# Cross-attention, 32 batches on one core: the first batch's split of queries and keys made by VectorE instead of accumulating transfers, and the set-up's order rewritten

## The chip, the core and the metric

The kernel runs on one core of a Trainium2 chip. The core has five engines with a queue of instructions each: PE (TensorE, matrix products into PSUM), DVE (VectorE), ACT (ScalarE), POOL (GpSimd) and SP (SyncE, which here only issues transfers). Each engine works through its queue in order and waits on semaphores for the others and for transfers. The metric is the device time of one execution in microseconds. All times below are in microseconds unless ns is written; those inside a profile count from the start of its span.

## The reference

`x` and `y` (called `ctx_2048`) are 32 x 256 x 1024 in float32, the weights 256 x 256. For each batch:

```python
x_q = einsum('oc,bcn->bno', w_qk, y)
x_k = einsum('oc,bcn->bon', w_qk, x)
x_v = einsum('oc,bcn->bon', w_v, x) + b_v
energy = einsum('bnc,bcm->bnm', x_q, x_k)            # 1024 x 1024
attention = softmax(energy, axis=-1)
attention = attention / (1e-07 + attention.sum(axis=1, keepdims=True))
x_r = einsum('bcn,bnm->bcm', x_v, attention)
x_r = relu(einsum('oc,bcn->bon', w_t, x - x_r) + b_t)
return x + x_r
```

Softmax runs over rows of the energy, the second normalisation over its columns.

## The kernel before

**Folded weights.** The energy is `y^T (w_qk^T w_qk) x`, so the kernel forms `G = w_qk^T w_qk` once (tile `g`) and per batch only `G x`, the *keys* (name `g` in tiles, class `Keys`). In the same way `w_t w_v` is folded into one matrix (tile `wvtT`, made by `value_weights`) for the *values* `u` (class `Values`), and `w_t` is turned by `turned_weights` (tile `wtT`). `value_bias` makes the bias `bu` of the values: DVE spreads `b_v` into `bvs` (inside `scratch`), PE multiplies (`pb`), ACT copies, and also negates `b_t` to `nbt`.

**Seven products.** Each product of 2 x 2 blocks is done with seven block products and not eight (class `Seven`). Block sums of the weights are made by DVE in `lefts` (tiles `gs`, `wtTs`, `wvtTs`, four scalar_tensor_tensor each, after ACT's copies of the PSUM banks), block sums of `x` in `summed` (tile `xs`: GpSimd's tensor_tensor for batch 0; for later batches two loads by SP and three accumulating transfers by GpSimd, `xsteps`). Three PSUM banks `one`, `two`, `three` collect the products: `p1`, `p5`, `p2` begin them; `p6`, `p7`, `p4` go on in `one`, `p3` in `two`. Between them ACT keeps copies (`p1s`, `p5s`, `w`). `c11`, `c12`, `c22` (DVE, one tensor_tensor of 128x512 each) and `c21` (an ACT copy) put the four blocks of the result together. For keys the result is `gfr`, two tiles of 128x1024 (block rows 0 and 1); for values it is `ut`. As all products but three go on in a bank that is read meanwhile, the order is tied: `p6` waits for the copy `p1s`, `p7` for the copy `w`, `p4` for `c22`'s reading, `c21` for `p4`.

**The split.** The energy needs more than one pass of the fast matrix form. Class `Split` keeps each of `y` (tile `yf`, from rows `yfr`) and the keys (tile `gf`, from `gfr`) in three forms of 128 x 2 x 1024 in fp32r: `high` (the value, scaled), `low` (what `high` lacks) and a third, `both`, that mixes the two. With `i` the block row, 0 or 1, `parts(i)` has ACT write `high`, and scaled copies of it to the places of `low` and `both`; `lower(i)` is a transfer of GpSimd's queue that adds the rows to `low`; `mixed(i)` is another that adds `low` to `both`, after the first has landed. So a batch has twelve ACT passes of 128x1024 and eight accumulating transfers of 512 KB.

**Energies.** Class `Energy` works on one of eight row tiles `n`. `products(h)` issues six matmuls `pe` of 128x512 for each half `h`: `high` by `high` and `low` by `low` into one bank, `both` by `both` into another, for `i` of 0 and 1. `gather(h)`: ACT scales the first bank into `es`, DVE's custom instruction adds the second bank, writes `e` and the running minimum `nm`. `exp` (ACT) follows one row later, `share` (DVE: a reciprocal and the addition into `acc`, the column sums) two rows later. After the last row, `columns` and `inverse` (DVE) make the column factors `rc`. Then class `Attention` scales `e` (DVE) and multiplies (PE, `po`). Before the attention of batch b the keys and values of batch b+1 are made, and their split.

**Order.** The class `InOrder` (lines 62 to 78) wraps PE, DVE, ACT and POOL so that each keeps the order in which the program is written; only waits move an instruction. SP's transfers go in the order written too. PSUM is one pool of eight banks, and buffers of `rowp` (four: the two `yfr` and two `gfr` of a batch) are reused when their last reader is done. So the order of the set-up, lines 631 to 673, is the order of every queue before the loop. At row 0 of batch 0 (lines 690 to 703) the values' `p4` and `c21` follow, then `xsteps[1]` and `[2]`, then `factors` on GpSimd: two additions of `bu` to `ut` and four block sums `us`.

In the trace all operations that go through `InOrder` carry one line (L73), so they are told apart by tiles.

Of the kernel before, what the change touches and what calls it, by code (L numbers as in the profile page):

```python
# [12 lines left out]
ALU = mybir.AluOpType  # L13
# [4 lines left out]
def kernel(  # L18
# [25 lines left out]
    KC = C // P  # L44
# [9 lines left out]
    UP = 4096.0  # L54
    UNDER = 1.0 - 2.0**-13
# [22 lines left out]
    pe, dve, act, pool = (InOrder(g) for g in (nc.tensor, nc.vector, nc.scalar, nc.gpsimd))  # L78

    def bank(name):  # L80
        return ps_m.tile([P, MB], F32, tag="m", name=name)
# [61 lines left out]
    def lefts(name, ps, sign=1.0):  # L143


        w = const.tile([P, KC, C], F32, name=name)
        for k in range(KC):
            act.mul(w[:, k, :], ps[k][:, :C], sign)
        sums = const.tile([P, 4, P], F32, name=f"{name}s")
        s1, s2, s3, s4 = (sums[:, j] for j in range(4))  # L150

        def stt(out_, block, factor, other, op):
            dve.scalar_tensor_tensor(out_, block, factor * sign, other, ALU.mult, op)

        p11, p12, p21 = ps[0][:, :P], ps[1][:, :P], ps[0][:, P:C]
        a11, a12, a21, a22 = w[:, 0, :P], w[:, 1, :P], w[:, 0, P:], w[:, 1, P:]
        stt(s1, p21, 1.0, a22, ALU.subtract)
        stt(s3, p11, 1.0, a21, ALU.subtract)
        stt(s2, p11, -1.0, s1, ALU.add)
        stt(s4, p12, 1.0, s2, ALU.add)  # L160
        return w, (a11, a12, s4, a22, s1, s2, s3)
# [10 lines left out]
    def turned_weights():  # L172

        pt = [bank(f"pt_{i}") for i in range(KC)]
        for i in range(KC):
            for k in range(KC):
                pe.transpose(pt[i][:, ts(k, P)], wt[:, k, ts(i, P)], ident)
        return lefts("wtT", pt)

    def value_weights(wtT):  # L180

        pw = [bank(f"pw_{i}") for i in range(KC)]
        for i in range(KC):
            for k in range(KC):
                pe.matmul(
                    pw[i][:, :C], wv[:, k, ts(i, P)], wtT[:, k, :], start=(k == 0), stop=(k == KC - 1)
                )
        return lefts("wvtT", pw, -1.0)[1]

    def value_bias(wtT):  # L190

        pb = bank("pb")
        for k in range(KC):
            dve.tensor_scalar(bvs[:, k], few, bv[:, k], None, ALU.add)
        for k in range(KC):
            pe.matmul(pb[:, :C], bvs[:, k], wtT[:, k, :], start=(k == 0), stop=(k == KC - 1))
        act.mul(bu.rearrange("p k c -> p (k c)"), pb[:, :C], -1.0)
        act.mul(nbt[:, :, 0], bt[:, :, 0], -1.0)
# [13 lines left out]
    def value(v):  # L212

        return v.bitcast(F32)

    def summed(b):

        s = up.tile([P, 4, MB], F32, tag="xs", name=f"xs_{b}")
        t1, t3, t4, t2 = (s[:, j] for j in range(4))
        to = loaded[b]  # L220
        b11, b12 = to[:, 0, ts(0, MB)], to[:, 0, ts(1, MB)]
        b21, b22 = to[:, 1, ts(0, MB)], to[:, 1, ts(1, MB)]
        if b == 0:
            pool.tensor_tensor(t1, b11, b12, ALU.add)
            pool.tensor_tensor(t2, b22, t1, ALU.add)
            pool.tensor_tensor(t3, b12, b22, ALU.add)
            pool.tensor_tensor(t4, b21, t2, ALU.add)
            steps = []
        else:
            q = quarters(x[b])  # L230
            nc.sync.dma_start(s[:, :2], q[:, 0, 1:2, :].to_broadcast([P, 2, MB]))
            nc.sync.dma_start(s[:, 2:], q[:, 1])
            steps = [
                lambda: accumulate(s[:, :2], corners(x[b])),
                lambda: accumulate(s[:, 2:], s[:, 0:1].to_broadcast([P, 2, MB])),
                lambda: accumulate(t4, q[:, 1, 1]),
            ]
        return (b11, b21, b22, t4, t1, t2, t3), steps

    class Split:  # L240
# [12 lines left out]
        def parts(self, i):  # L253

            high, low, both = (self.to[:, j, i] for j in range(3))
            act.mul(high, self.rows[i], UNDER * self.by)
            act.mul(low, value(high), -1.0 / self.by)
            act.mul(both, value(high), -1.0 / (UP * self.by))

        def lower(self, i):  # L260
            accumulate(value(self.to[:, 1, i]), self.rows[i])
# [370 lines left out]
    q = Queries(0)  # L632
# [4 lines left out]
    g = Keys(0, xr)  # L637
    g.p1()
    g.p5()
    g.p2()  # L640
    g.p6()
    wtT, t_left = turned_weights()
    g.p3()
    g.p7()
    u_left = value_weights(wtT)
    value_bias(wtT)
    for i in range(KC):
        q.parts(i)
        q.lower(i)
    g.c11()  # L650
    g.c12()
    g.split.parts(0)
    g.split.lower(0)
    g.c22()
    g.p4()
    g.c21()
    g.split.parts(1)
    g.split.lower(1)
    for i in range(KC):
        q.mixed(i)  # L660
        g.split.mixed(i)
    xn, xsteps = summed(1)
    xsteps[0]()
    u = Values(0, xr)
    u.p1()
    u.p5()
    u.p2()
    u.c11()
    u.p6()
    u.p3()  # L670
    u.c12()
    u.p7()
    u.c22()

    before = None
    for b in range(B):
# [34 lines left out]
        if more:  # L711
            q = Queries(b + 1)
            for i in range(KC):
                q.load(i, nc.sync.dma_start)
            g = Keys(b + 1, xn)
# [33 lines left out]
        if more:  # L749
# [33 lines left out]
            xr, u = xn, un  # L783
# [34 lines left out]
```

## Time and profile before

| what | value |
|---|---|
| time, median of 3 runs | 2130.79 (2130.71 to 2130.84) |
| the profiled execution's own time | 2130.66 |
| its span | 2128.9 |
| mean granted clock of PE | 0.994 |
| first pe matmul | 35.39 |
| pe running without a break, from the second row on | 52.44 |
| first matmul of batch 1's keys | 71.80 |
| first matmul of batch 2's keys | 139.51 |
| first matmul of batch 3's keys | 204.91 |

The span runs from the first to the last recorded instruction of the execution. A row such as `L73 PE MATMUL pe<-gf,yf 128*128 128x512 f32 x3072` is a group: engine, operation, the tile written and the tiles read, sizes, and how many. In an answer in order of time the two numbers ahead are start and length; several like instructions may be merged in one row (then `x` tells how many), and brackets at the end tell how long the engine stood still before it and what released it. In a row on waits the numbers are the total, how often, and the longest.

### The profile page before, as it was taken

The page shows a single profiled execution, that of the slowest core. Times are in us where ns is not written, and L with a number is a line of the kernel's source. Part 1 is how long each engine was busy: PE and PEld are TensorE (multiplying, and loading weights), DVE is VectorE, ACT ScalarE, POOL GpSimd, SP SyncE. Part 2 cuts the span into 40 slices and gives each one's busy share as a digit, 9 for nine tenths or more (in the row PEclk, how much of TensorE's full clock was granted, in tenths as well). Part 3 has the DMA queues.
Part 4 walks back from the last instruction along what each step waited for, and adds up shares of the span by engine and source line. Part 5 has one row for each costly group of instructions (what it writes and reads, how often), then busy time and mean ns, then how long its engine had stood idle before and what let it go on. Part 6 is the DMA issues. An engine that isn't in the chain of part 4 may idle for free.

```text
span 2128.9 us, 23494 instructions
## 1 busy us (share of the span) xinstructions
PE 2087.1 (98%) x7586; PEld 1290.6 (61%) x7586; DVE 1812.7 (85%) x3024; ACT 1179.7 (55%) x1802; POOL 681.3 (32%) x582
## 2 busy tenths in 40 slices
PE   5999999999999999999999999999999999999998
PEld 4666556665556665566655566655666555666564
DVE  1988889888899888898888998888888889988898
ACT  3664556655556645566555566455665555664562
POOL 2333331333332333323333323333233333233321
PEclk7999999999999999999999999999999999999999
DMA  8456766557766567665577665676655776656740
GB/s 206 88 127 163 177 154 129 139 136 181 168 128 145 129 163 178 155 133 134 136 179 167 128 146 128 163 178 150 135 138 135 177 170 127 148 127 162 178 95 30
DMA packets 108954, 310.34 MB, mean 146 GB/s; under 512 B 10784, under 2 KB 11552, under 8 KB 108832
## 3 DMA queue, kind: packets, MB, share of 16 engines
q0 software_dynamic: 58192, 174.87, 44.9%
q1 hardware_dynamic: 50496, 133.85, 18.5%
q8 instruction: 60, 0.98, 0.2%
q14 instruction: 62, 0.51, 0.1%
q10 hardware_dynamic: 144, 0.13, 0.0%
HBM read 124.78 MB, written 33.55 MB: 74 GB/s over the span
## 4 chain that ended last, share of the span: by engine, by line
PE 61%; DVE 29%; issue 4%; ACT 1%; DMA 1%; DVEq 0%; POOL 0%; ACTq 0%; POOLq 0%
PE pe L73 31%; PE po L73 28%; DVE e L73 14%; DVE acc L73 4%; DVE et L73 4%; DVE gfr L73 3%; DVE rc L73 2%; DVE sc L73 1%; PE pu L73 1%; DVE parts L73 1%; ACT es L73 1%; DVE ri L73 0%; DMA gf<-gfr 0%; PE pg L73 0%; DMA gf<-gf 0%
## 5 line engine op out<-in xcount | busy, mean ns | idle before, releaser
L73 PE MATMUL pe<-gf,yf 128*128 128x512 f32 x3072 | 718.7, 394 | 10.9 <-DMA gf<-gf 10.9
L73 PEld LDWEIGHTS pe<-gf,yf 128*128 128x128 f32 x3072 | 578.0, 188 | 145.7 <-issue 27.3
L73 ACT ACTIVATE es<-pe 128x512 f32<-128x512 f32 x512 | 304.2, 595 | 184.7 <-PE pe L73 184.4
L73 PE MATMUL po<-et,us 128*128 128x512 f32 x768 | 353.9, 597 | 11.5 <-DVE et L73 11.5
L73 DVE SCALAR_TENSOR_TENSOR e<-e,ri,rc 128x512 f32<-128x512 f32 x512 | 347.4, 746 | 1.1
L73 DVE SCALAR_TENSOR_TENSOR acc<-e,ri,acc 128x1024 f32<-128x1024 f32 x224 | 289.9, 1294 | 8.0
L73 ACT ACTIVATE e<-e,nm 128x1024 f32<-128x1024 f32 x256 | 292.7, 1143 | 3.4 <-DVE nm L73 3.3
L73 PEld LDWEIGHTS po<-et,us 128*128 128x128 f32 x768 | 142.9, 190 | 207.0 <-issue 158.4
L73 DVE CUSTOM_DVE_ANT_0 e<-pe,es,nm 128x512 f32<-128x512 f32 x256 | 192.2, 751 | 76.5 <-ACT es L73 49.4
L73 PE MATMUL po<-e,ut 128*128 128x512 f32 x512 | 225.0, 592 | 1.0 <-DVE e L73 1.0
L73 POOL DMA_DIRECT2D yf<-yfr x64 | 55.0, 860 | 533.0 <-ACT yf L73 518.6
L73 DVE CUSTOM_DVE_ANT_0 e<-pe,es 128x512 f32<-128x512 f32 x256 | 175.5, 686 | 51.6 <-ACT es L73 39.1
L73 ACT ACTIVATE z<-po,bt 128x512 f32<-128x512 f32 x31 | 21.4, 689 | 337.1 <-DMA out_dram<-z 234.5
L73 PEld LDWEIGHTS po<-e,ut 128*128 128x128 f32 x512 | 97.2, 190 | 123.8 <-issue 107.4
L73 DVE TENSOR_TENSOR et<-e 128x1024 f32<-128x1024 f32 x128 | 153.7, 1221 | 4.4
L73 POOL TENSOR_TENSOR ut<-ut,bu 128x1024 f32<-128x1024 f32 x64 | 153.5, 2473 | 0.0
L73 POOL DMA_DIRECT2D gf<-gf x64 | 54.8, 856 | 306.3 <-DMA gf<-gfr 262.8
L73 DVE SCALAR_TENSOR_TENSOR z<-z,x 128x512 f32<-128x512 f32 x96 | 132.2, 1377 | 3.3
L73 ACT ACTIVATE yf<-yf 128x1024 fp32r<-128x1024 f32 x128 | 128.2, 1049 | 2.0
L73 ACT ACTIVATE gf<-gf 128x1024 fp32r<-128x1024 f32 x128 | 128.2, 1049 | 2.0
L73 PE MATMUL po<-e,us 128*128 128x512 f32 x256 | 125.3, 592 | 0.0
L73 POOL DMA_DIRECT2D xs<-xs x31 | 37.2, 1201 | 248.4 <-DMA xs<-in_x_dram 240.9
(106 smaller groups left out, 2753.7 us busy)
## 6 DMA issues: line engine op xcount, KB each, us to landing
yfr<-in_ctx_dram SPq DMA_DIRECT2D x64, 512.0 KB, 5.8
yf<-yfr POOLq DMA_DIRECT2D x64, 512.0 KB, 5.1
gf<-gfr POOLq DMA_DIRECT2D x64, 512.0 KB, 10.6
yf<-yf POOLq DMA_DIRECT2D x64, 512.0 KB, 8.0
gf<-gf POOLq DMA_DIRECT2D x64, 512.0 KB, 5.2
out_dram<-z SPq DMA_DIRECT2D x128, 256.0 KB, 3.5
x<-in_x_dram SPq DMA_DIRECT2D x31, 1024.0 KB, 7.4
xs<-in_x_dram SPq DMA_DIRECT2D x62, 512.0 KB, 5.1
```

The source lines that it names most:

```text
L73: self.last = getattr(self.engine, name)(*args, **kwargs)
```

## The change

Only code ahead of the loop changes, for batch 0; batches 1 to 31 are issued as before. `Split` gets three new methods. `high(i)` is the ACT pass for `high` as before. `low(i)` is one DVE scalar_tensor_tensor of 128x1024 (`high` times a constant, plus the rows), written straight to the `low` form; `both(i)` is another (`high` times a constant, plus `low`). In the set-up they take the place of `parts`, `lower` and `mixed`: eight ACT passes and eight transfers go, eight DVE instructions come.

The order changes too. The keys' `c11`, `c12`, `c22`, `p4` and `c21` move ahead of `value_weights`, with the passes `high` of `y` among them; `value_weights` stands behind the passes `high` of the keys; the remaining `low` and `both` follow its block sums on DVE; `value_bias` moves behind the values' products `p1` to `p7`; the values' `c11` and `c12` move behind it. `xsteps[0]` on GpSimd's queue is no longer behind eight transfers.

```diff
+        def high(self, i):
+            act.mul(self.to[:, 0, i], self.rows[i], UNDER * self.by)
+
+        def low(self, i):
+            high, low = (self.to[:, j, i] for j in range(2))
+            dve.scalar_tensor_tensor(
+                low, value(high), -1.0 / self.by, self.rows[i], ALU.mult, ALU.add
+            )
+
+        def both(self, i):
+            high, low, both = (self.to[:, j, i] for j in range(3))
+            dve.scalar_tensor_tensor(
+                both, value(high), -1.0 / (UP * self.by), value(low), ALU.mult, ALU.add
+            )
...
     g.p1()
     g.p5()
     g.p2()
+    g.c11()
+    q.high(0)
     g.p6()
+    q.low(0)
     wtT, t_left = turned_weights()
     g.p3()
+    q.high(1)
+    g.c12()
     g.p7()
-    u_left = value_weights(wtT)
-    value_bias(wtT)
-    for i in range(KC):
-        q.parts(i)
-        q.lower(i)
-    g.c11()
-    g.c12()
-    g.split.parts(0)
-    g.split.lower(0)
     g.c22()
+    q.low(1)
     g.p4()
     g.c21()
-    g.split.parts(1)
-    g.split.lower(1)
+    g.split.high(0)
+    g.split.high(1)
+    u_left = value_weights(wtT)
     for i in range(KC):
-        q.mixed(i)
-        g.split.mixed(i)
+        g.split.low(i)
+    for i in range(KC):
+        g.split.both(i)
+    for i in range(KC):
+        q.both(i)
     xn, xsteps = summed(1)
     xsteps[0]()
     u = Values(0, xr)
     u.p1()
     u.p5()
     u.p2()
-    u.c11()
     u.p6()
     u.p3()
+    u.p7()
+    value_bias(wtT)
+    u.c11()
     u.c12()
-    u.p7()
     u.c22()
```

## The prediction

> **What bounds the kernel now.** I read the page first, then the stretches of the set-up, then who waited for whom in it, then the instructions in order of time. The page says that the loop is TensorE's:
>
> ```profile
> PE 2087.1 (98%) x7586; PEld 1290.6 (61%) x7586; DVE 1812.7 (85%) x3024; ACT 1179.7 (55%) x1802; POOL 681.3 (32%) x582
> PEclk7999999999999999999999999999999999999999
> ```
>
> 98% busy, and the granted clock is low only in the first of 40 slices (53 us each): what PE lost lies there, the set-up that the change rewrites. Cut into stretches (span, then busy time and count of PE, PEld, DVE, ACT, POOL, then clock, DMA share, GB/s):
>
> ```profile
> 24.00:35.00 11.00, 4.75 (x22) 4.76 (x23) 1.38 (x2) 7.17 (x10) 4.33 (x5) 0.57 1.03 233
> 35.00:53.00 18.00, 8.02 (x26) 6.06 (x26) 2.15 (x5) 1.37 (x3) 3.29 (x3) 0.60 0.85 157
> 53.00:72.00 19.00, 19.00 (x85) 15.75 (x84) 14.86 (x29) 14.04 (x26) 12.11 (x7) 1.00 0.21 34
> ```
>
> From 24 to 53 us PE is less than half busy at about half clock while the DMA engines are full; from 53 us it never stops. The waits up to 75 us say on what:
>
> ```profile
> PE pe L73 <- DMA gf<-gf: 9.9, 2, 5.4
> PE pu L73 <- ACT up1s L73: 8.8, 1, 8.8
> POOL yf L73 <- ACT yf L73: 11.2, 2, 9.2
> ```
>
> and in order of time (start, length):
>
> ```profile
> 24.12 2.00 ACT L73 ACTIVATE gf<-gf 128x1024 fp32r<-128x1024 f32 x2
> 29.63 0.57 ACT L73 COPY up1s<-pu 128x512 f32<-128x512 f32 x1
> 36.98 0.86 POOL L73 DMA_DIRECT2D gf<-gf  x1 [2.37 <-DMA gf<-gfr]
> 41.55 0.77 PE L73 MATMUL pe<-gf,yf 128*128 128x512 f32 x1 [4.49 <-DMA gf<-gf]
> 47.76 3.32 PE L73 MATMUL pe<-gf,yf 128*128 128x512 f32 x7 [5.44 <-DMA gf<-gf]
> 52.44 19.51 PE L73 MATMUL pe<-gf,yf 128*128 128x512 f32 x84
> 59.50 2.52 DVE L73 TENSOR_SCALAR acc<-e,ri 128x1024 f32<-128x1024 f32 x1
> 81.36 1.25 DVE L73 TRANSPOSE_TENSOR_REDUCE parts<-acc 128x32 f32<-128x1024 f32 x1
> ```
>
> ACT is a chain from 17.09 to 29.7 (twelve passes of 1.05 over yf and gf); GpSimd's transfers wait for its passes (the third wait), and PE's pu waits behind it for one copy, 8.8 us. Then the energies pe wait for the eight accumulating transfers, the last landing just before 47.7. From 52.44 PE runs 84 matmuls (seven rows of twelve, 0.2305 us each) to 71.80, where the next batch's keys begin.
>
> **The change, part by part.**
>
> *Removed:* eight transfers and eight of ACT's passes (8.4 us). With them go PE's 9.9 us of waiting on gf and nearly all of the 8.8 us behind up1s. What is late next is VectorE, which receives eight scalar_tensor_tensor of 128x1024 with two SBUF operands. The nearest row is that of acc<-e,ri,acc: 1.28 us undisturbed, 1.96 and 1.84 at 63.67 and 67.29 beside GpSimd's tensor_tensor. From 12 us to the end of the chain GpSimd only issues transfers, so I take 1.28 for one and 1.20 from start to start (ten of half the size take 6.71, that is 0.67 each for a duration of 0.746).
>
> [...]
>
> *The new chain.* Its first wait is new: ACT's high(0) stands ahead of the copy gw, and yfr_0 lands at 12.3 (issued at 4.14, 8.2 to landing), yfr_1 at 13.5.
> - ACT: high(0) 12.3-13.4, gw to 14.0 (0.59; was over at 10.6), wtT twice to 14.7, high(1) to 15.8.
> - PE: p3 ends at 11.2 as before; p7 goes onto the bank that gw reads, so it moves from 11.1 to 14.05-15.1.
> - DVE: low(0) 13.4-14.7, the four wtTs sums (1.1) to 15.9, c12 and c22 (0.62 apart) to 17.15, low(1) to 18.4. c11 is done by 9.9, in idle time.
> - PE: p4 waits for c22: 17.2. Then pw.
> - ACT: c21 (0.57), the two high passes of gf (2.1), only then the two wvtT copies (0.38 each).
> - DVE: the wvtTs sums (1.1) stand ahead of the six remaining scalar_tensor_tensor, so these wait for wvtT. After them two bvs (0.47); value_bias's matmuls pb need bvs, and every pe is queued behind pb.
>
> *The clock.* Before, a stretch without work at 22.2-25.6 was followed by clock 0.50 from 25.6; a stretch with 1.16 of 3.41 us busy (35.85-39.26) by 0.50; one with 1.83 of 3.37 busy (12.0-15.37) left it at 1.00; a full one (32.4-35.85) brought it back. New gaps: between 11.2 and 17.2 PE does only p7 (1.0 us), and between the end of pu and pb nothing. By these rows both cost half clock afterwards; I take that.
>
> [...]
>
> With half clock: p4 17.2-19.2 and pw (1.89 full, 3.8 half) to 22.7; c21 to 19.8, high of gf to 22.0, wvtT to 22.4 and 23.1; wvtTs to 24.25; six times 1.20 to 31.5; bvs to 32.0. Meanwhile pu, six products 0.9 apart from 22.4, is over by 28, with idle time after it. pb at half clock (1.9) ends at 33.9. Row 0 (twelve pe) then has 1.95 us at half clock, 4.2 matmuls, and 7.8 at 0.231: 37.65. u's p4 (0.9): 38.55. Seven rows, 19.36: **57.9 instead of 71.80, 13.9 us earlier.**
>
> With full clock throughout: pw over at 20.1, wvtT at 21.7, wvtTs 22.8, six to 30.0, bvs 30.5, pb 31.4, row 0 34.2, p4 35.1, rows 54.5: 17.3 earlier. This is the good end. The bad end is VectorE at 1.96 eight times: 5.4 later, 8.5 earlier than now.
>
> *What the rows gain besides.* In the first batch VectorE trailed PE more than later: from the start of the keys (71.80) to the column reduction (81.36) 9.56 us, in the next batch 7.25 (139.51, 146.76). The distance between key starts is 67.71 for the first and 65.40 for the second: the trail cost PE 2.3. Its source is GpSimd, whose six tensor_tensor of u's factors (56.35 to 68.05) stretched acc to 2.52, 1.96 and 1.84 (the means of these forms are 0.81 and 1.29). They start after u's c21. Before, GpSimd was held until 56.35 by the xs accumulations queued behind the eight transfers; now those can go at 18 and are over by about 33, so the factors start at about 39.5, some 3 us earlier against the rows, and cover one share and part of another. Between nothing and 2.3 I take 1.0.
>
> *Costed at nothing:* c11, under the wait for yfr. The next batch's yfr loads, whose slots are freed by low(0) and low(1) instead of the transfers: needed at 83 only, they now start near 18.7 behind xs on SP's queue. nbt and bu move behind pu; bu is due when GpSimd adds it at 39.5 and is over by about 35. If PE ran faster than here, this would be the next wait, off PE's path. u's c11, c12 and c22 (2 us) follow bvs, to 34.2; only u's p4 at 37.65 waits for c22. PSUM: at row 1 a bank may have to wait for u's c21 (0.59), with the first sums' matmuls as cover; 0 to 0.6.
>
> *Sum:* 13.9 + 1.0 = 14.9. The profiled execution took 2130.66 (span 2128.9 and 1.8 around it), against a median of 2130.79, so both are one base: 2130.66 - 14.9 = 2115.8. Say **2116**.
>
> **The rivals.**
> 1. *The clock holds* (other phase, or p7 enough). For: 54% busy kept it. Against: 1.0 in 6 us is far less. 17.3 + 0 to 2.3: 2111 to 2113.
> 2. *VectorE or the queue order costs more*: contention, later yfr, half clock for a stretch more (3.4 us at half, 1.7 lost), no recovered trail. 2118 to 2122.
> 3. *The rows become VectorE's.* A row costs it 0.69 + 0.08 + 0.75 + 0.08 + 0.16 + 1.28 = 3.04 of work against PE's 2.77. Before, it had idle time ahead of row 0; now it comes out of the set-up with u's three sums. If the trail grows by its full 0.27 a row and GpSimd's stretch (2.9) stays whole, 5 of the gain go: 2121. Against: steady batches run so with a trail of 7.
> 4. *Slower.* One mechanism: scalar_tensor_tensor on VectorE stretched 3.2-fold, as z<-z,x at 178.69 shows (2.22 where 0.69 is usual, beside GpSimd). Eight at 4.1 instead of 1.28 add 22.6: 2138. It decides from 3.7 us each (14.9 + 4.3, over eight, on top of 1.28). Against: that row lies beside a tensor_tensor of GpSimd, and the transfers that GpSimd issues from 96.05 to 98.1 leave TENSOR_TENSOR et at 96.29 at 1.23.
> 5. *The transfers were hidden anyway*: no change. PE's 9.9 us wait names them, with 8.8 more behind ACT; little is left for it.
>
> **How the numbers follow.** Forecast (2114 to 2118) 0.55, rival 1 0.15, rival 2 0.16, rival 3 0.07, rival 4 0.04, no change 0.03. A measurement of this kernel tells about 0.2%, 4.3 us. The first four are all faster: 0.93; same 0.03; slower 0.04. The range takes in rival 1 from its full recovery and rivals 2 and 3 to 2121.5, and leaves out the rest: 2111.5 to 2121.5.
>
> **What the profile after would show.** Eight scalar_tensor_tensor of about 1.28 on yf and gf; six of them between 24 and 32; no wait of pe on DMA; ACT idle from 8.9 to 12.3 before yf<-yfr; first pe near 34, continuous to the keys near 58; clock below 1 in the stretches after 15 and after 32; column reduction about 8.5 after the start of the keys, and 65 to 67 from there to the next. The forecast is wrong if the new passes take over 2 us, if pe still stops between rows, or if a gain at 58 is given back by batch 1.

## The result, and the profile after

The changed kernel takes 2112.91 us (median of four executions, 2108.64 to 2113.70) against 2130.75 for the kernel before measured beside it (2130.5 to 2130.84): a ratio of 0.9913, 95% interval 0.9898 to 0.9929. That is 17.8 us less, where 14.9 were forecast. The median lies inside the forecast range of 2111.5 to 2121.5; the execution that was profiled, at 2108.64, lies below it.

From the page of the changed kernel, its engine totals and its clock row:

```profile
PE 2081.3 (99%) x7586; PEld 1286.3 (61%) x7586; DVE 1815.0 (86%) x3032; ACT 1171.9 (56%) x1794; POOL 673.3 (32%) x574
PEclk9999999999999999999999999999999999999999
```

Eight instructions left ACT and eight left GpSimd, eight came to DVE. The clock row alone settles little, since a 9 stands for 0.90 or more; but the mean granted clock of this execution is 1.00, and no part of its first 40 us shows less. The stretches of the set-up, in the columns used before (span; busy time and count of PE, PEld, DVE, ACT, POOL; clock; DMA share; GB/s):

```profile
24.00:35.00 11.00, 8.26 (x49) 7.17 (x49) 7.91 (x14) 3.44 (x7) 5.52 (x4) 1.00 0.44 73
35.00:53.00 18.00, 18.00 (x79) 14.61 (x78) 15.20 (x35) 14.30 (x26) 6.98 (x5) 1.00 0.00 1
53.00:72.00 19.00, 19.00 (x81) 11.36 (x80) 18.33 (x33) 15.29 (x22) 2.58 (x3) 1.00 0.32 55
```

From 35 to 53 us PE was busy for 8.0 us before and is busy for all 18 now, with the DMA engines at rest. Who waited for whom up to 62 us (total, how often, longest):

```profile
DVE wvtTs L73 <- ACT wvtT L73: 3.2, 1, 3.2
PE pb L73 <- DVE scratch L73: 2.7, 1, 2.7
PE pg L73 <- DVE gfr L73: 1.9, 1, 1.9
ACT yf L73 <- DMA yfr<-in_ctx_dram: 1.8, 1, 1.8
PE pg L73 <- ACT gw L73: 1.1, 1, 1.1
PE pu L73 <- ACT wvtT L73: 1.1, 1, 1.1
```

PE's 9.9 us of waiting on transfers of `gf` and its 8.8 us behind `up1s` are gone. What it waits for in their place is small: `p7` for `gw`, `p4` for `c22` (written to `gfr`) and `pb` for VectorE's `bvs` (in `scratch`), all three named in the prediction, and `pu` for `wvtT`. In order of time (start, length):

```profile
11.56 1.06 ACT L73 ACTIVATE yf<-yfr 128x1024 fp32r<-128x1024 f32 x1 [1.84 <-DMA yfr<-in_ctx_dram]
13.23 1.10 PE L73 MATMUL pg<-xs,gs 128*128 128x512 f32 x2 [1.13 <-ACT gw L73]
16.20 1.10 PE L73 MATMUL pg<-xs,g 128*128 128x512 f32 x2 [1.87 <-DVE gfr L73]
21.33 2.35 DVE L73 SCALAR_TENSOR_TENSOR gf<-gf,gfr 128x1024 fp32r<-128x1024 f32 x2
23.59 2.35 DVE L73 SCALAR_TENSOR_TENSOR gf<-gf 128x1024 fp32r<-128x1024 f32 x2
25.87 2.35 DVE L73 SCALAR_TENSOR_TENSOR yf<-yf 128x1024 fp32r<-128x1024 f32 x2
28.56 1.10 PE L73 MATMUL pb<-wtT,scratch 128*128 128x256 f32 x4 [2.74 <-DVE scratch L73]
30.54 2.73 POOL L73 TENSOR_TENSOR ut<-ut,bu 128x1024 f32<-128x1024 f32 x1
33.05 19.30 PE L73 MATMUL pe<-gf,yf 128*128 128x512 f32 x84
39.90 1.09 DVE L73 TENSOR_SCALAR acc<-e,ri 128x1024 f32<-128x1024 f32 x1
52.19 1.02 PE L73 MATMUL pg<-x,g 128*128 128x512 f32 x2
59.10 1.25 DVE L73 TRANSPOSE_TENSOR_REDUCE parts<-acc 128x32 f32<-128x1024 f32 x1
```

The chain is the one in the prediction, link by link: landing of `yfr`, copy `gw`, `p7`, `c22`, `p4`, then VectorE's six forms back to back from 21.33 to 28.14, `pb`, rows. The keys of batch 1 start at 52.19 (before: 71.80), 19.61 earlier. The distance to the next keys (117.25) is 65.06 instead of 67.71, another 2.65. Together 22.26; this execution is 2130.66 - 2108.64 = 22.02 shorter than the profiled one of before. So in this execution the whole gain is made before 117 us; of a lead of 22.4 at the keys near 1030 us, 22.0 is left at the end.

### The profile page after: what moved, and what is told of

Its sections match the earlier page's. It is cut to its first block, busy times and chain, and to the rows that moved or that the text cites. A ratio compares the mean times of both kernels' runs of the same rounds, so it can differ in the third digit from the quotient of the medians.

```text
span 2106.9 us, 23473 instructions
## 1 busy us (share of the span) xinstructions
PE 2081.3 (99%) x7586; PEld 1286.3 (61%) x7586; DVE 1815.0 (86%) x3032; ACT 1171.9 (56%) x1794; POOL 673.3 (32%) x574
## 4 chain that ended last, share of the span: by engine, by line
PE 62%; DVE 29%; issue 4%; ACT 1%; DMA 1%; DVEq 0%; POOL 0%; ACTq 0%; POOLq 0%
PE pe L73 31%; PE po L73 29%; DVE e L73 14%; DVE acc L73 4%; DVE et L73 4%; DVE gfr L73 3%; DVE rc L73 2%; DVE sc L73 1%; PE pu L73 1%; DVE parts L73 1%; ACT es L73 1%; DVE ri L73 0%; DMA gf<-gfr 0%; PE pg L73 0%; DMA gf<-gf 0%
```

## The experiments

All ran against the kernel before on the same chip. The first four share a chip (before: 2130.62), e5 to e8 another (2130.88), e9 a third (2131.35). Unless the text says otherwise, times are medians of four executions. `e1_again` and `e8_again` are the changed kernel itself, so that the others have it on their own chip.

The columns to compare, each from the profiled execution (for "trail": from the keys of batch 1 to the column reduction `parts<-acc`; the last three columns are the first three `share` on `acc`, which take 0.75, 1.28 and 1.28 where GpSimd does not stretch them):

| kernel | time | keys of batch 1 | to the keys of batch 2 | trail | first shares |
|---|---|---|---|---|---|
| before | 2130.75 | 71.80 | 67.71 | 9.56 | 2.52, 1.96, 1.84 |
| changed | 2112.91 | 52.19 | 65.06 | 6.91 | 1.09, 1.29, 1.28 |
| e1_again | 2111.57 | 55.45 | 65.01 | 6.88 | 1.07, 1.28, 1.28 |
| e2_filled | 2109.10 | 51.77 | 65.86 | 7.70 | 1.45, 1.29, 1.28 |
| e3_held_factors | 2114.79 | 56.03 | 67.85 | 9.75 | 2.72, 1.95, 1.84 |
| e4_old_order | 2113.40 | 57.04 | 65.03 | 6.89 | 1.05, 1.28, 1.28 |
| e5_order_transfers | 2128.14 | 69.59 | 68.04 | 9.91 | 2.88, 1.95, 1.84 |
| e6_both_early | 2109.07 | 50.86 | 66.15 | 8.01 | 1.63, 1.84, 1.28 |
| e7_best | 2106.44 | 46.68 | 67.83 | 9.70 | 2.65, 1.96, 1.84 |
| e8_again | 2110.84 | 54.08 | 65.06 | 6.91 | 1.09, 1.28, 1.28 |
| e9_best_factors | 2104.27 | 46.98 | 65.84 | 7.71 | 1.90, 1.28, 1.28 |

### The same kernel again: where is the half clock?

No edit. The first profile had a clock of 1.00 throughout, which the prediction held for the less likely case; its three other executions had a mean granted clock of 0.997.

> The changed kernel as it is, timed more often, because its four runs lie apart (2108.64, 2112.44, 2113.39, 2113.70) where the kernel before lies within 0.4 us. Theory A (the clock): TensorE's clock falls to half in the set-up in some runs and not in others, by where windows of 3.41 us fall against the gaps of the set-up; then times form two groups, about 2108.6 with a mean granted clock of 1.000 and 2112 to 2114 with about 0.997 (0.3% of 2111 us are 6.3 us lost to the clock scale, that is about 12 us at half clock), and a profile with 0.997 shows the half clock between 15 and 40 us. Theory B (the landing of x and yfr): times spread evenly with the landing of yfr_0 and the clock has no part in it; then runs of one clock lie apart by some us as well.

Measured: 2111.57 (2109.94 to 2112.81), ratio 0.9909 [0.9894, 0.9924]; the profiled execution took 2112.81 at a mean clock of 0.998. Its stretches:

```profile
17.00:20.50 3.50, 3.50 (x7) 2.17 (x8) 0.84 (x1) 1.57 (x3) 1.35 (x1) 0.54 0.64 208
27.00:34.00 7.00, 4.25 (x14) 3.33 (x14) 5.01 (x8) 0.80 (x3) 2.66 (x3) 0.76 0.59 95
13.40:17.00 3.60, 1.25 (x3) 0.48 (x4) 3.50 (x8) 1.84 (x4) 0.00 (x0) 0.97 1.03 399
27.00:30.40 3.40, 0.65 (x5) 0.49 (x5) 3.40 (x6) 0.00 (x0) 0.19 (x1) 1.00 0.86 149
```

and PE's instructions there:

```profile
16.85 2.05 PE L73 MATMUL pg<-xs,g 128*128 128x512 f32 x2 [1.88 <-DVE gfr L73]
18.69 2.65 PE L73 MATMUL pw<-wtT,scratch 128*128 128x256 f32 x8
30.17 1.77 PE L73 MATMUL pb<-wtT,scratch 128*128 128x256 f32 x4 [2.75 <-DVE scratch L73]
31.37 4.29 PE L73 MATMUL pe<-gf,yf 128*128 128x512 f32 x12
```

The two half-clock stretches are where the prediction put them: after the gap around `p7` (`p4` takes 2.05 instead of 1.10), and after the gap ahead of `pb` (row 0 takes 4.29 instead of 3.10). But each lasts about 3.4 us, so the first ends near 20.2, inside `pw`: `pw` takes 2.65, not 3.8. The keys start at 55.45, which is 3.26 later than with full clock and 2.45 earlier than the forecast of 57.9.

### The gaps of PE filled

```diff
+    def fill(p, count):
+        for _ in range(count):
+            pe.matmul(p[:, :P], few, few, start=True, stop=True)
...
+    pw = [bank(f"pw_{i}") for i in range(KC)]
+    fill(pw[0], 5)
     g.p7()
+    fill(pw[1], 7)
...
         pb = bank("pb")
+        fill(pb, 11)
```

The extra products multiply a tile of zeros (`few`); what they write is overwritten by `pw` and `pb`.

> As the changed kernel, with small matmuls of zeros (128x128) put into TensorE's three gaps: 5 ahead of the keys' p7, 7 ahead of p4, 11 ahead of pb, into banks that the next product starts anew. Theory A: the clock stays at 1.000 in every run, and all times lie at 2108 to 2110 (up to 1 us more than the best run if the fillers overrun a gap). Theory B: the spread of 5 us stays.

Measured: 2109.10 (2108.88 to 2109.63), ratio 0.9899 [0.9882, 0.9915], with a clock of 1.00 in all four executions. The two stretches that cost e1 its clock:

```profile
13.40:17.00 3.60, 3.33 (x20) 2.42 (x19) 3.23 (x8) 0.86 (x2) 0.43 (x1) 1.00 1.04 404
27.00:30.40 3.40, 3.13 (x18) 2.61 (x17) 3.02 (x6) 0.69 (x3) 0.00 (x0) 1.00 0.90 154
```

PE is now busy for 3.33 of 3.60 and 3.13 of 3.40 (in e1: 1.25 and 0.65), and the clock stays. The spread shrinks from 2.9 us in e1 to 0.75, and the median falls by 2.5. So the gaps cause the half clock, and the half clock most of the spread. Over the twelve executions of the changed kernel (first result, e1, e8) the times go with the mean clock: at 1.0 2108.64, 2109.58 and 2109.94; at 0.998 six between 2110.81 and 2112.81; at 0.997 2112.44, 2113.39 and 2113.70. Three of twelve executions kept the clock without any filling.

### The factors held back

```diff
-                if b == 0:
-                    ur, usteps = u.factors()
-                    for step in usteps:
-                        step()
...
+            if b == 0 and n == 1:
+                pool.tensor_copy(behind, e[:, 1, N - 1 : N])
+                ur, usteps = u.factors()
+                for step in usteps:
+                    step()
```

GpSimd's six tensor_tensor then start only when row 1 of the energies is written, which is the relation to the rows that the kernel before had.

> As the changed kernel, with GpSimd's factors of the first batch held until row 1 of the energies has been gathered, by one copy of a column of e ahead of them. Theory T (the trail): the shares beside GpSimd stretch as in the kernel before (acc 2.52, 1.96, 1.84), the column reduction stands about 9.5 us after the start of the keys and not 6.9, and the time is 2.2 to 2.7 us above the changed kernel in runs of the same clock. Rival: the trail has another cause (VectorE came later to row 0); then nothing changes, within 0.5 us.

Measured: 2114.79 (2111.64 to 2115.16), ratio 0.9921 [0.9907, 0.9936], 3.2 slower than e1 (its one execution at a clock of 1.0 took 2111.64, that of e1 2109.94). In order of time, GpSimd's additions and VectorE's first three shares:

```profile
41.11 4.79 POOL L73 TENSOR_TENSOR ut<-ut,bu 128x1024 f32<-128x1024 f32 x2
43.73 2.72 DVE L73 TENSOR_SCALAR acc<-e,ri 128x1024 f32<-128x1024 f32 x1
47.68 1.29 POOL L73 TENSOR_TENSOR us<-us,ut 128x512 f32<-128x512 f32 x1
48.11 1.95 DVE L73 SCALAR_TENSOR_TENSOR acc<-e,ri,acc 128x1024 f32<-128x1024 f32 x1
48.94 2.27 POOL L73 TENSOR_TENSOR us<-ut 128x512 f32<-128x512 f32 x1
51.17 1.30 POOL L73 TENSOR_TENSOR us<-ut,us 128x512 f32<-128x512 f32 x1
51.71 1.84 DVE L73 SCALAR_TENSOR_TENSOR acc<-e,ri,acc 128x1024 f32<-128x1024 f32 x1
65.78 1.25 DVE L73 TRANSPOSE_TENSOR_REDUCE parts<-acc 128x32 f32<-128x1024 f32 x1
```

The stretched shares of before are back, the second and third almost to the hundredth (2.72, 1.95, 1.84 against 2.52, 1.96, 1.84), with them the trail (9.75) and the distance to the next keys (67.85, 2.84 more than in e1). This is the second part of the gain, made and unmade by the time at which GpSimd's additions run. Another 0.58 stands already ahead of the keys (56.03 against 55.45): the profiled execution of e3 has one 3.4 us stretch of half clock more than that of e1.

### The forms by VectorE in the old order

```diff
-    g.c11()
-    q.high(0)
     g.p6()
-    q.low(0)
     wtT, t_left = turned_weights()
     g.p3()
-    q.high(1)
+    g.p7()
+    u_left = value_weights(wtT)
+    value_bias(wtT)
+    for i in range(KC):
+        q.high(i)
+        q.low(i)
+    g.c11()
     g.c12()
-    g.p7()
+    g.split.high(0)
+    g.split.low(0)
     g.c22()
-    q.low(1)
     g.p4()
     g.c21()
-    g.split.high(0)
     g.split.high(1)
-    u_left = value_weights(wtT)
-    for i in range(KC):
-        g.split.low(i)
-    for i in range(KC):
-        g.split.both(i)
+    g.split.low(1)
     for i in range(KC):
         q.both(i)
+        g.split.both(i)
...
     u.p2()
+    u.c11()
     u.p6()
     u.p3()
+    u.c12()
     u.p7()
-    value_bias(wtT)
-    u.c11()
-    u.c12()
     u.c22()
```

This is the order of before, with `high`, `low` and `both` in the places of `parts`, `lower` and `mixed`.

> The order of the set-up as in the kernel before, with the low and third forms by VectorE (high, low and both in the place of parts, lower and mixed, no transfers). If the forms alone make the gain: within 1 us of the changed kernel. If the order matters as I work it out: ACT is free for the high forms at 17, c22 stands behind two to three of VectorE's passes, p4 starts near 24.7 and the last form is done near 33, against 28.1 in the changed kernel's profile: 3.5 to 6 us slower than the changed kernel in the same clock, about 2112 to 2117.

Measured: 2113.40 (2113.2 to 2113.8), ratio 0.9918 [0.9904, 0.9933]: 17.2 faster than before, 1.8 slower than e1. PE in order of time:

```profile
25.57 2.05 PE L73 MATMUL pg<-xs,g 128*128 128x512 f32 x2 [8.14 <-DVE gfr L73]
33.93 3.13 PE L73 MATMUL pe<-gf,yf 128*128 128x512 f32 x12
57.04 1.02 PE L73 MATMUL pg<-x,g 128*128 128x512 f32 x2
```

and two stretches of its set-up:

```profile
17.00:24.00 7.00, 0.42 (x2) 0.02 (x1) 3.96 (x5) 3.42 (x5) 1.45 (x2) 0.69 0.64 137
24.00:29.00 5.00, 3.44 (x10) 2.43 (x11) 1.42 (x2) 1.32 (x2) 1.11 (x1) 0.50 0.93 237
```

`p4` comes 8.7 us later than in e1 (25.57 against 16.85), yet the keys only 1.6 later (57.04 against 55.45). The old order makes `pw` and `pb` while it waits, so that after `p4` only `pu` stands ahead of the energies; in the new order `wvtT`, its block sums, six forms and `pb` follow `p4`. My expectation of 3.5 to 6 us counted the wait and too little of what it covers. The long wait has a price of its own: the clock is at half from 19.7 to 29.9, over `p4` and into the values' products, so the 1.8 is no difference at equal clock, for which the expectation was made. The forms, put into the old order, make nearly all the gain.

### The new order with the transfers

```diff
-    q.high(0)
+    q.parts(0)
+    q.lower(0)
     g.p6()
-    q.low(0)
...
-    g.split.high(0)
-    g.split.high(1)
+    g.split.parts(0)
+    g.split.lower(0)
+    g.split.parts(1)
+    g.split.lower(1)
     u_left = value_weights(wtT)
     for i in range(KC):
-        g.split.low(i)
-    for i in range(KC):
-        g.split.both(i)
-    for i in range(KC):
-        q.both(i)
+        q.mixed(i)
+        g.split.mixed(i)
```

> The new order of the set-up with the old forms: parts, lower and mixed (ACT's passes and eight accumulating transfers) where the changed kernel has high, low and both. Theory F (the forms make the gain, the order little): ACT's twelve passes again stand ahead of wvtT and the transfers go one after another, from about 15 to 42 us, so pe stops on gf as before and the trail of 9.5 us is back: 2123 to 2128. Rival (the order makes the gain): within 4 us of the changed kernel, 2109 to 2116.

Measured, ten executions: 2128.14 (2126.38 to 2129.5), ratio 0.9986 [0.9976, 0.9995]: 2.7 faster than before, 17.3 slower than e8 on the same chip. Its rows of PE and GpSimd in order of time:

```profile
32.96 1.20 POOL L73 DMA_DIRECT2D yf<-yf  x1
35.18 0.86 POOL L73 DMA_DIRECT2D gf<-gf  x1 [1.02 <-DMA gf<-gfr]
39.73 0.47 PE L73 MATMUL pe<-gf,yf 128*128 128x512 f32 x1 [1.41 <-DMA gf<-gf]
45.91 3.32 PE L73 MATMUL pe<-gf,yf 128*128 128x512 f32 x7 [5.70 <-DMA gf<-gf]
```

PE waits 7.1 us for `gf<-gf` (before: 9.9): the last transfer is issued at 35.2 and lands just before 45.9. The forms bring 17.2 in the old order (e4) and 17.3 in the new one (e5 against e8); the order brings 2.7 with the transfers and 1.8 with the forms. So neither needs the other to work. The edit takes the transfers and eight of ACT's passes away together, and no run has one without the other, so their shares in the 17 us are not shown apart. The rows of e5 point to the transfers: ACT's last pass over `gf` is done at 28.41 (26.41, length 2.00), 17.5 us before the last landing.

### Rows earlier: `both` of `y` ahead of `value_weights`

```diff
     g.split.high(1)
+    for i in range(KC):
+        q.both(i)
     u_left = value_weights(wtT)
     for i in range(KC):
         g.split.low(i)
     for i in range(KC):
         g.split.both(i)
-    for i in range(KC):
-        q.both(i)
```

In the changed kernel VectorE stands idle for 3.2 us ahead of `wvtTs`; two forms fit there.

> As the changed kernel, with VectorE's two passes that make the third form of y put ahead of the value weights' block sums, into the 3.2 us in which VectorE waits for wvtT. If the chain wvtT, wvtTs, six passes, bvs, pb sets the start of pe, as I work it out, it becomes four passes: pe starts 2.3 us earlier (27.0 where the profile at full clock had 29.31), the gap ahead of pb nearly closes (2.7 to 0.5 us), so that the clock falls less often; 2106 to 2107 at full clock, median 2106 to 2110. If pu or another chain sets it: no change at full clock.

Measured: 2109.07 (2107.64 to 2109.91), ratio 0.9896 [0.9882, 0.9911], 1.8 faster than e8. The energies start at 27.98 (changed kernel: 29.31) and the keys at 50.86, 1.33 before those of the first result, where 2.3 were expected (one half-clock stretch is left, `p4` taking 2.04); the next keys at 117.01, only 0.24 before. The lead is spent in the rows: GpSimd starts its factors at 31.80, held by the last `xs` accumulation ahead of them, while the rows have moved forward, and two shares are stretched to 1.63 and 1.84.

### A shorter set-up throughout

The order of e7 spreads `b_v` early, makes `value_bias` between `p7` and `p4`, puts ACT's `high` of `y` behind the copies that `p7` and `wtT` need, and makes three forms of `y` in VectorE's idle time ahead of `wvtT`'s block sums:

```diff
     g.c11()
-    q.high(0)
     g.p6()
-    q.low(0)
-    wtT, t_left = turned_weights()
+    spread_bias()
+    wt_copies = turned_weights()
     g.p3()
-    q.high(1)
     g.c12()
     g.p7()
+    q.high(0)
+    q.high(1)
     g.c22()
-    q.low(1)
+    wtT, t_left = wt_copies()
+    value_bias(wtT)
     g.p4()
     g.c21()
+    q.low(0)
     g.split.high(0)
     g.split.high(1)
+    q.low(1)
+    q.both(0)
     u_left = value_weights(wtT)
...
-    for i in range(KC):
-        q.both(i)
+    q.both(1)
...
     u.p7()
-    value_bias(wtT)
     u.c11()
```

`spread_bias` is the DVE part of `value_bias`; `wt_copies` is `turned_weights` without its block sums, which `wt_copies()` makes.

> A version drawn from the profiles: ACT's gw and wtT copies ahead of the high forms of y (so no copy waits for yfr), c12 and c22 ahead of wtT's block sums, bvs and the bias's product pb in the early gaps, one third form of y ahead of wvtT's block sums. Expected: p4 near 14, wvtT near 18, the last form done near 25.3 and pe from there (29.3 or 31.4 in the profiles of the changed kernel), no gap of TensorE over 1.5 us, so clock 1.0 in all runs: about 2104.5, 2103 to 2106, and a spread below 1 us. If the clock's threshold is passed all the same: 2107 to 2109.

Measured: 2106.44 (2106.3 to 2106.92), ratio 0.9885 [0.987, 0.99], with a clock of 1.00 in all four: 0.4 above the 2103 to 2106 expected. The keys start at 46.68, 5.51 before those of the first result, but the next only 2.74 before. In order of time:

```profile
31.36 5.12 POOL L73 TENSOR_TENSOR ut<-ut,bu 128x1024 f32<-128x1024 f32 x2
34.39 2.65 DVE L73 TENSOR_SCALAR acc<-e,ri 128x1024 f32<-128x1024 f32 x1
38.69 1.96 DVE L73 SCALAR_TENSOR_TENSOR acc<-e,ri,acc 128x1024 f32<-128x1024 f32 x1
```

It is e3 over again: the rows came forward by 5.5 us, GpSimd's factors stayed, and now cover three shares. Half of the lead is lost there.

### And its factors moved forward

```diff
                     xsteps[1]()
-                    xsteps[2]()
...
                 if b == 0:
                     ur, usteps = u.factors()
                     for step in usteps:
                         step()
+                    xsteps[2]()
```

One accumulating transfer of `xs` moves behind the factors on GpSimd's queue; all else is e7.

> As e7_best, with the third accumulation of xs issued by GpSimd behind the first batch's factors and not ahead of them. In e7_best the factors start at 31.36, held by the accumulations, and the first three shares take 2.65, 1.96 and 1.84, from the keys of batch 1 to those of batch 2 67.83 us. Theory T (the trail is made by GpSimd's factors beside the shares): the factors start at 26.5 to 27.5, the shares shrink to about 1.6, 1.5 and 1.28, the distance to 65.5 to 66.5, the time to 2104.5 to 2105. Rival (the trail grows because PE comes earlier, whatever GpSimd does): distance and time as in e7_best, 67.8 and 2106.4.

Measured: 2104.27 (2103.35 to 2104.61), ratio 0.9872 [0.9856, 0.9889]; before on that chip 2131.35. It is faster than both kernels, and by 27.1 us faster than the one before. In order of time:

```profile
26.81 5.22 POOL L73 TENSOR_TENSOR ut<-ut,bu 128x1024 f32<-128x1024 f32 x2
34.68 1.90 DVE L73 TENSOR_SCALAR acc<-e,ri 128x1024 f32<-128x1024 f32 x1
38.23 1.28 DVE L73 SCALAR_TENSOR_TENSOR acc<-e,ri,acc 128x1024 f32<-128x1024 f32 x1
```

The factors start 4.55 us earlier, one share instead of three is touched, and the distance between the keys falls from 67.83 to 65.84.

### The changed kernel beside e5 to e7

> The changed kernel once more, beside these. Theory A: each run lies either at 2108 to 2109 (clock 1.000) or at 2111 to 2114 (clock 0.997 or 0.998), and a profile at half clock shows it behind the gaps ahead of p4 and pb.

Measured: 2110.84 (2109.58 to 2111.64), ratio 0.9905 [0.989, 0.992]. Profiled at 2110.87: again two half-clock stretches (`p4` 2.04, row 0 3.99), the keys at 54.08, the trail 6.91. Its `p7` starts at 12.53, in e1 at 13.88, in the first profile at 13.23: the landing of `yfr` moves the chain by up to 1.35 us from one execution to the next.

## Why the prediction was right, and where its sizes were off

**The mechanism held.** Faster was right (0.93). The transfers' landing was the wait (e5 keeps the transfers, and ACT's passes with them, and keeps the wait), VectorE does come next, and PE runs without a break into the keys. Measured against the steps of the forecast, on the two profiles that stand for its two cases:

| step | forecast, half clock | e1_again | forecast, full clock | changed, first profile |
|---|---|---|---|---|
| first `high` starts | 12.3 | 12.20 | 12.3 | 11.56 |
| `p4` starts | 17.2 | 16.85 | 17.2 | 16.20 |
| `pw` over | 22.7 | 21.34 | 20.1 | 19.02 |
| first of six forms starts | 24.25 | 22.93 | 22.8 | 21.33 |
| `bvs` starts | 31.5 | 29.74 | 30.0 | 28.14 |
| `pb` over | 33.9 | 31.94 | 31.4 | 29.66 |
| seven rows start | 38.55 | 36.31 | 35.1 | 33.05 |
| keys of batch 1 | 57.9 | 55.45 | 54.5 | 52.19 |

**The term "p4 17.2-19.2 and pw to 22.7" was too large.** It let the half clock run through all of `pw`. The stretch lasted 3.4 us and ended inside it, so `pw` was over 1.36 early, of which 0.35 was there already at `p4`. That is the largest single error of the half-clock chain, though not all of it reached the forms: in e1 ACT takes `wvtT` at 21.32 straight behind its `high` passes, without waiting for `pw`. By e1's rows `pw` at half clock throughout (18.69 to 22.5) would have ended `wvtT` about 0.9 later than the 21.97 measured. The rest came in small pieces: the six forms at 1.135 from start to start, not 1.20 (0.44 over six), `bvs` and `pb` 0.2, row 0 with `u`'s `p4` 0.3, the seven rows 19.14 instead of 19.36. In sum 2.45. With full clock the landing of `yfr` was 0.74 early besides. That the median lies inside the range rests on three of its four executions having half clock; the fourth lies below it.

**The term "between nothing and 2.3 I take 1.0" was too small.** The distance between the keys fell by 2.65, more than the upper bound, and in half-clock and full-clock profiles alike (65.01 to 65.06). The step that failed is "the factors start at about 39.5". They started at 30.54 in the first profile and at 32.44 in e1. I had put them behind `u`'s `c21`, since they stand behind it in the program. But the first addition of `bu` reads only block row 0 of `ut`, which `c11` and `c12` write, so it waits for `bu` (in e1, 32.35) and for the `xs` accumulations ahead of it on GpSimd's queue (in the first profile, the last issued at 29.95). GpSimd is through before the second share; e3 shows what the other case costs. The bound of 2.3 compared the first batch with the next one's 65.40; but the fourteen distances that follow the first in the kernel before average 65.06 ((1050.3 - 139.5) / 14), so that one was itself still 0.3 too long.

**Rival 1 was underpriced in gain.** "1.0 in 6 us is far less" spoke against a clock that holds. It held in 3 of 12 executions, the profiled one among them; that neither confirms nor refutes a chance of 0.15. Its first reason, another phase, fits the profiles: the same gaps cost two stretches of half clock in e1 and in e8 and none in the first profile. Its price, 2111 to 2113, was too high by the same early links as above (52.19 instead of 54.5 for the keys) and by the trail: the three such executions took 2108.64 to 2109.94. They lie below the range, which was to take in this rival from its full recovery but by the prediction's own terms began 0.4 above it (2130.66 - 17.3 - 2.3 is 2111.1).

**Half clock is no single case.** The forecast took both gaps at half clock. Twelve executions gave a mean clock of 0.997, 0.998 or 1.0, and times from 2108.64 to 2113.70. The half-clock executions (2110.81 to 2113.70) stand 2.3 to 5.2 below the forecast of 2116; the two errors named, 2.45 for the chain and 1.65 for the trail, come to 4.1.

**The other rivals.** VectorE's forms were not stretched (last section), which takes away rival 4 and most of rival 2. Rival 3 needs a growing trail; it shrank to 6.9, and the seven rows took 19.14. Rival 5 falls with e4: without the transfers, and in the old order, 17.2 us go.

**Not expected: how little the order does.** The prediction worked the chain out for both edits together. Apart, the forms bring 17.2 and the order 1.8 to 2.7. The waits of `p4` and `pb` that the order removes or makes lie on either side of nearly the same length of work.

## What to carry to other kernels

In this short set-up an accumulating transfer cost far more by its landing (in e5 the last one of `gf`, issued at 35.18, landed just before 45.91) than the vector instruction in its place (1.21 to 1.22): look at what the bounding engine waits for, and not at how busy the DMA engines are. When a set-up is shortened, follow the engine that has its own queue through the same stretch: here GpSimd's additions took half of the 5.5 us that e7 gained in the set-up, and e9 won most of that back. What released them was their data and what stood ahead of them on GpSimd's own queue; that ACT's `c21` stands ahead of them in the program held them back for the second addition only (0.73 us behind ACT's `ut` at 34.01 in the first profile). The changed kernel, with gaps of about two to three us on TensorE in its set-up (1.98, 1.88 and 2.75 in e1), had several times, not one (2108.64 to 2113.70); with the gaps filled (e2) its times lay within 0.75. Fill such gaps before comparing small edits.

## What the runs showed of the hardware

**The granted clock.** In e1 a stretch of 3.60 us with 1.25 of PE work (13.4 to 17.0) and one of 3.40 with 0.65 (27.0 to 30.4) were each followed by about 3.4 us at half clock, in which TensorE was busy throughout, and then by full clock. Where TensorE was not busy throughout, half clock stayed longer: 6.8 us in e3 (15.06 to 21.89, busy for 1.63 of the first 3.41), 10.2 us in e4 (19.67 to 29.91, with nothing and then 0.93 in the first two stretches of 3.41). The two half-clock stretches begin 13.65 us apart in e1 (16.8 and 30.4) and in e8 (15.2 and 28.8) and 17.07 apart in e3 (15.06 and 32.13), four and five times 3.41; the kernel before had half clock for 10.25 us (25.60 to 35.85) and for 13.66 (39.26 to 52.92), three and four times 3.41. (Where a stretch begins and ends is worked out from the mean clock of the windows around it.) The same gaps, a little shifted, cost nothing in the first profile: with 1.54 of 3.41 us busy (13.65 to 17.06) and 0.66 of 3.40 (25.6 to 29.0) the clock stayed at 1.00. Stretches in which TensorE was busy for a third of the time (e1, 1.25 of 3.60), and in e3 for 1.35 of 3.41 us (28.72 to 32.13), were enough to lose the clock, where 1.83 of 3.37 in the kernel before (12.0 to 15.37) were not. So the busy share of a stretch alone does not tell whether the clock is lost.

**VectorE beside GpSimd.** While GpSimd only issued transfers, a form of 128x1024 took 1.21 to 1.22 us on VectorE; from the group rows of the first profile between 9 and 36 us:

```profile
L73 DVE SCALAR_TENSOR_TENSOR yf<-yf,yfr 128x1024 fp32r<-128x1024 f32 x2 | 2.4, 1222 | 1.9 <-ACT yf L73 1.9
L73 DVE SCALAR_TENSOR_TENSOR gf<-gf 128x1024 fp32r<-128x1024 f32 x2 | 2.4, 1215 | 0.0
```

Beside GpSimd's tensor_tensor the shares went from 1.28 to 1.84 and 1.96, and the first, 0.75 in most batches (median of the 32 in the first profile), to as much as 2.88. How long a share takes follows from when GpSimd's instruction ends. In e3 the additions of `bu` end at 45.90 and the first share at 46.45; `us<-us,ut` ends at 48.97 and the second share at 50.06; `us<-ut,us` ends at 52.47 and the third share at 53.55. All 20 stretched shares of the first batch, in the eleven profiles, end so: the first 0.54 to 0.56 and a later one 1.07 to 1.09 after the GpSimd instruction beside it, which is 0.2 less than each takes alone. The shares look as if held until that instruction is over, and GpSimd's next one is held in turn (2.27 instead of 1.30 at 48.94). So the cost in these rows is what is left of one GpSimd instruction, and no factor on VectorE's work, as rival 4 of the prediction priced it (3.2-fold): that rival's own row, `z<-z,x` at 178.69, ends 0.55 after the additions of `bu` beside it (180.91 and 180.36). The rows show the stretch beside GpSimd's tensor_tensor and none beside its transfer issues: the two `gf<-gf` from 23.59 to 25.94, with an issue from 24.60 to 25.80 beside them, took 1215 ns each. The first share has a single tensor input of 128x1024 (`acc<-e,ri`) and was stretched the most (2.88 for 0.75 in e5).

**What the clock moved.** In the first profile the keys are 19.61 us earlier, in e1 16.35; yet both have 65.0 us to the next keys. The half clock cost time in the set-up only, and the rows up to the next keys were the same. (In e1 a lead of 19.05 at those keys is 17.85 at the end; nothing here tells why.)
